# Two halves for the last dense tile of each batch, and other settings for the last five jobs of a planned decoder layer

## The chip, the core and the metric

The kernel runs on one core of a Trainium2 chip. The core has a matrix engine (TensorE, PE in the profile, with its weight loads shown apart as PEld), a vector engine (VectorE, DVE), a scalar engine (ScalarE, ACT), a general engine (GpSimd, POOL) and a queue that issues the transfers here (SyncE, SP). Each engine works through its own list of instructions in order; semaphores tie the lists together. The metric is the device time of one execution in microseconds, as the median of several runs.

## The reference, cut to what matters

The layer works on x of 2 batches by 512 tokens by 1024 features and has three parts, each a residual around a normalised input: an attention with weights cut to their signs, a second attention over a 256-wide stream with a gated block behind it ("xattn"), and a dense layer with low-rank additions ("ffn").

```python
x = x + attn(layernorm(x), ...)
x = x + xattn(layernorm(x), pos, ctx, ...)
x = x + ffn(layernorm(x), gate, kernel, bias, lora_A, lora_B, lora_A_shared, lora_B_shared)

def ffn(x, ...):
    base_out = x @ kernel + bias                    # 1024 x 1024
    A_eff = einsum('bn,nri->bri', gate, lora_A)     # rank 32, mixed per batch
    B_eff = einsum('bn,nor->bor', gate, lora_B)
    delta = B_eff (A_eff x) + lora_B_shared (lora_A_shared x)
    return base_out + delta
```

The change is in the last part and in what precedes it directly. There the output of a tile of 128 tokens is: the normalised tile times the 1024x1024 weights (into which the shared low-rank product is added beforehand), plus the mixed low-rank product, plus the bias, plus the tile itself.

## The kernel before, in words

The kernel is written as some thirty jobs, Python generators that yield one step at a time: an engine, an estimated time, and the moment at which the step's inputs are ready. A planner, `run` (line 453), keeps a clock for each engine and always takes the step with the smallest sum of possible start and lag. The instructions of that step are emitted then, and on each engine they stay in the order in which they were emitted. So the plan fixes the order of all work when the kernel is built; on the chip each instruction then starts when its semaphores allow.

The lag is a priority in microseconds: a job with lag -1.0 is put ahead of a step that could start at the same moment with lag 0.5. The list in `build` (line 1669) gives each job its generator, its lag, and the names that must be finished before it begins. A job's side steps (a copy out of PSUM, a sum, a store) are spawned as jobs of their own, with a lag relative to their parent's: `LAGS` (line 432), looked up first as "job.function" and then as "function", -0.3 if neither is there. `lined` (1205) starts the tiles of a job in order, at most so many at a time, and adds 0.02 of lag per tile.

Buffers are counted in rooms: `take` waits until one is free in the plan, `give` returns it. There are 12 slabs of 8 KB per partition, 4 probs of the same size, 8 pages and 11 rows in SBUF, and 3 pairs (two banks of 512 columns) and 2 single banks in PSUM. At most 3 tail tiles run at once (three lanes). All transfers are issued on SP, in planned order (`fetch`, 535).

The jobs that the change touches, letters A and B standing for batch 0 and 1:

- attC and attD: the second attention of each batch. attC's end gives back three slabs, attD's end three more.
- `factors_back` (job factorsB, 1519): loads the mixed low-rank factors, which an earlier job put into DRAM, into two slabs with six transfers: 1024 KB, 512 KB and four of 128 KB.
- `dense_weights` (job weights, 1536): loads the shared factors and the bias into three pages; then, for each quarter of the 1024x1024 weights, loads 1024 KB into a probs or slab buffer, forms the shared low-rank product of that quarter in two PSUM pairs and adds it on VectorE (`joined`).
- `tails` and `tail` (1369, 1376): for each of four tiles of 128 tokens per batch the rest of the second part: a write of the attention into the stream (`write`, 1257), a read, the gated block (`gated`), a second write, and the addition of the residual, which is loaded again (`residual`). The write has a long chain of small VectorE operations.
- `dense_all` and `dense` (1580, 1583): the third part, tile by tile, two at once per batch. A dense tile begins when weights and factorsB are done and its tail is done. It measures and normalises the tile (VectorE), turns it on TensorE in eight blocks into xt, copies it out, forms the mixed rank product ax, spawns `summed` (which folds the four partial sums of ax), and multiplies into one PSUM pair: 8 products of 512 columns for each of two halves h (each product appears as two records in the profile). Then one rank product for each half closes the pair, one VectorE operation adds the pair to the tile with its bias into a page y, and one transfer of 512 KB stores y.

`SPARE` (446) is read in one place, `attend` (734): in the first attention, the last of four probability tiles of a group is summed directly by TensorE, not added to the others on VectorE first, when VectorE is planned to be busy for longer than SPARE after the product, and always in the last group.

Of the kernel before, what the change touches and what calls it, by code (L numbers as in the profile page):

```python
# [15 lines left out]
ALU = mybir.AluOpType  # L16
AX = mybir.AxisListType

P = 128
NB = 2  # L20
S = 512
NT = S // P
D = 1024
# [46 lines left out]
class Kernel:  # L70
# [354 lines left out]
    def output_weights(self):  # L425
# [6 lines left out]
    LAGS = {  # L432
        "added": 0.0, "ahead": 0.0, "attA.ahead": -0.1, "attA.exponentials": -0.1, "attA.finished": 0.3,
        "attB.added": 0.0, "attB.ahead": -0.3, "co.emptied": -0.1, "cv.emptied": -0.1, "denseA.emptied": -1.0,
        "denseA.summed": -0.6, "denseB.emptied": 0.3, "denseB.summed": -2.0, "emptied": -0.6,
        "exponentials": 0.3, "factor.put": -1.0, "finished": 0.0, "gained": -1.0, "gated": -1.0,
        "joined": -0.6, "k.scale_of": 0.0, "maxA.reduced": 0.0, "maxA.turned": -0.1, "maxB.reduced": 0.3,
        "maxB.turned": -0.3, "maxD.turned": -0.3, "outA.clean": 1.0, "outA.stored": 2.0, "outB.stored": -1.0,
        "proj0.featured": -1.0, "proj0.valued": -0.6, "proj1.featured": -1.0, "proj1.valued": -0.6,
        "q.scale_of": 0.0, "residual": 1.0, "rotated": 0.0, "stateA.emptied": -0.3, "stateA.rotated": -0.1,  # L440
        "stateB.gained": 0.0, "stateB.rotated": 0.0, "stored": 0.6, "summed": -0.6, "tableB.emptied": -2.0,
        "tailA.gained": -1.0, "tailA.residual": -2.0, "tailB.emptied": -0.6, "tailB.gained": -2.0,
        "tailB.gated": -0.6, "tailB.residual": 0.3, "v.scale_of": 0.0, "weights.joined": -0.1,
        "wo.scale_of": 0.0,
    }
    SPARE = 0.5

# [168 lines left out]
    def attend(self, groups, operands, scale, causal):  # L618
# [89 lines left out]
        for n, (g, kt) in enumerate(steps):  # L708
# [23 lines left out]
            else:  # L732

                direct = kt == NT - 1 and (g == groups - 1 or self.free["DVE"] > t + self.SPARE)
                if held is not None and not direct:
# [122 lines left out]
    def stored(self, b, q, x, halves):  # L858
        t = yield from self.join(*halves)
        t = yield from self.fetch(self.kept[b][q][:, :], x, 512, t)  # L860
        self.give("page", t)
        self.when[f"kept{b}{q}"] = t
        return t
# [719 lines left out]
    def dense(self, b, q, tails):  # L1583

        nc = self.io
        weights = yield from self.need("weights", "factorsB")
        t = yield from self.need(f"{tails}.{q}")
        xs = self.tokens(b, q)
        mv, r, t = yield from self.measured([[xs[:, :512], xs[:, 512:]]], t)
        t = max(t, (yield from self.take("page", 2)))  # L1590
        t = yield "DVE", 0.82, t
        xn = self.page([P, D])
        xt = self.page([P, ND, P])
        nc.vector.tensor_scalar(xn, xs, mv[:, 0, 0:1], r, ALU.subtract, ALU.mult)

        def biased(t):
            t = yield "DVE", 1.22, t
            nc.vector.tensor_tensor(xs, xs, self.bias, ALU.add)
            return t

        bias = self.spawn(biased(t), 1.0)
        ends = []
        for g in range(2):
            room = yield from self.take("bank")
            done = yield "PE", 0.62, max(t, room)
            turns = self.transposes(xn, g)
            ends.append(self.spawn(self.emptied("bank", xt[:, 4 * g : 4 * g + 4, :], turns, 512, done)))
        self.give("page", done)
        t = yield from self.join(*ends)
        t = max(t, weights)  # L1610


        r = (NT * b + q) * 32
        slots = [slice(32 * j, 32 * j + 32) for j in (q, q ^ 1)]
        both = slice(64 * (q // 2), 64 * (q // 2) + 64)
        ready = t
        t = max(t, (yield from self.take("row")), (yield from self.take("bank")))
        ax = self.row([P, 2, P])
        t = yield "PE", 0.6, t
        bank = self.bank([P, P])  # L1620
        for i in range(ND):
            j = 32 * (i % 4)
            self.mm(bank[j : j + 32, :], lhsT=self.ae[:, i, r : r + 32], rhs=xt[:, i, :], start=i < 4, stop=i >= 4)

        def summed(bank, t):
            t = yield "DVE", 0.3, t
            nc.vector.tensor_copy(ax[:, 0, :], bank)
            self.give("bank", t)
            t = max(t, (yield from self.take("bank")))
            t = yield "PE", 0.25, t  # L1630
            bank = self.bank([P, P])
            self.mm(bank[both, :], lhsT=self.eyes, rhs=ax[:, 0, :], start=True, stop=True)
            t = yield "DVE", 0.25, t
            nc.vector.tensor_copy(ax[both, 1, :], bank[both, :])
            self.give("bank", t)
            return t

        ranks = self.spawn(summed(bank, t))
        ready = max(ready, (yield from self.take("pair")))
        pair = self.pair()  # L1640
        for h in range(2):
            for i0 in range(0, ND, 2):
                t = yield "PE", 1.82, ready
                for i in range(i0, i0 + 2):
                    self.mm(
                        pair[:, h, :], lhsT=xt[:, i, :], rhs=self.wk[2 * h + i // 4][:, i % 4, :],
                        start=i == 0, stop=False,
                    )
        t = yield "PE", 0.6, max(t, (yield from self.join(ranks)))
        for h in range(2):  # L1650
            self.mm(
                pair[:, h, :], lhsT=ax[slots[h], 1, :], rhs=self.be[slots[h], b, h * 512 : (h + 1) * 512],
                start=False, stop=True,
            )
        self.give("page", t)
        self.give("row", t)
        t = max(t, (yield from self.join(bias)), (yield from self.take("page")))
        t = yield "DVE", 1.22, t
        y = self.page([P, D])
        nc.vector.tensor_tensor(  # L1660
            y.rearrange("p (h n) -> p h n", h=2), pair, xs.rearrange("p (h n) -> p h n", h=2), ALU.add
        )
        self.give("pair", t)
        t = yield from self.fetch(self.out[b * S + q * P : b * S + (q + 1) * P, :], y, 512, t)
        self.give("page", t)
        return t


    def build(self):
# [41 lines left out]
                ("stateB", self.state_inputs(1, False), 0.5, "outB"),  # L1711
                ("factor", self.factors(), -0.5, "maxB.3"),
                ("attC", self.attend_2(0, "maxC"), 0.2, "maxC.0"),
                ("factorsB", self.factors_back(), 5.0, "attD"),
                ("maxD", self.peaks_2(1, "stateB"), 0.5, "stateB", "attC.scores"),
                ("tailW", self.tail_weights(), -0.5, "attC", "stateB"),
                ("tailA", self.tails(0), 0.5, "attC", "tailW"),
                ("attD", self.attend_2(1, "maxD"), 0.2, "maxD.1"),
                ("weights", self.dense_weights(), 0.0, "attD", "attC"),
                ("tailB", self.tails(1), 0.0, "attD", "tailW", "tailA.0"),  # L1720
                ("denseA", self.dense_all(0, "tailA"), 0.5, "tailA.0"),
                ("denseB", self.dense_all(1, "tailB"), 0.2, "tailB.0"),
            ]
        )

# [103 lines left out]
```

## Time and profile before

| what | value |
|---|---|
| median of 3 runs | 1134.14 us (1129.55 to 1135.88) |
| profiled execution | 1131.76 us, of it 1130.0 us of span |
| TensorE | 1050.0 us busy (93%), mean granted clock 0.964 |
| VectorE | 842.0 us busy (75%) |
| ScalarE / GpSimd | 443.7 us (39%) / 239.3 us (21%) |
| DMA | 70.51 MB, mean 62 GB/s |

The span runs from the first to the last instruction in the profile; the rest of the profiled execution's time lies around it. An execution is read by stage: attC ends near 711 us, attD near 845, the dense weights are joined between 849 and 869, and the dense tiles run from 869 to the end, beside the remaining tail tiles. A busy TensorE is not TensorE at full speed: the granted clock tells what share of the full rate it had. Idle time of an engine is named by what ended it, behind an arrow. A row of a timeline has start and duration in us, engine, line, operation, what is written and read, and shapes; L51, L130, L133 and L142 are lines of helpers that record all VectorE, ScalarE and GpSimd operations, matmuls, transposes and transfers, so operations are told apart by the names of their tiles. A tile's name begins with the job that made it: the tokens of batch 0 lie in `tailA_slab` from the tail to the dense stage.

### The profile page before, as it was taken

Reading aid. Unit: us, or ns where it says so; the run is one execution under the profiler, and the core shown is the slowest. Engines: PE = TensorE matmul, PEld = TensorE weight load, DVE = VectorE, ACT = ScalarE, POOL = GpSimd, SP = SyncE. Lnnn points to the kernel's source line nnn. Section 1 sums busy time; section 2 is a strip of 40 time slices with the busy share of each in tenths; the row PEclk is TensorE's granted clock in tenths of the full one; section 3 lists DMA queues with packets and bytes.
Section 4 is the critical chain, followed back from the end, with each engine's and each line's share of the span. In section 5 each row is a group of like instructions: output and inputs, shape, how many; then the busy total and the mean of one; then the engine's idle time right before and its main releaser. Section 6 shows DMA issues by size and latency. Waiting matters only on the chain.

```text
span 1130.0 us, 16083 instructions
## 1 busy us (share of the span) xinstructions
PE 1050.0 (93%) x6331; PEld 520.9 (46%) x6364; DVE 842.0 (75%) x1391; ACT 443.7 (39%) x712; POOL 239.3 (21%) x249
## 2 busy tenths in 40 slices
PE   4889999999999998999999899989987899999897
PEld 3554353333233542332554553546455466675543
DVE  8968888478888866778777972499758778777582
ACT  6763101389600113787221256225753233332310
POOL 3542323412221403264452012001210000000000
PEclk9999999999998897999999899969999899999999
DMA  6621000100213321150022100510143011010100
GB/s 245 213 82 29 20 10 14 35 20 20 66 38 125 137 75 38 26 204 1 17 78 74 49 11 1 187 39 1 47 148 124 0 57 57 23 71 1 56 19 38
DMA packets 25232, 70.51 MB, mean 62 GB/s; under 512 B 5298, under 2 KB 5316, under 8 KB 24260
## 3 DMA queue, kind: packets, MB, share of 16 engines
q1 hardware_dynamic: 25156, 69.48, 18.2%
q8 instruction: 50, 0.82, 0.3%
q14 instruction: 26, 0.21, 0.1%
HBM read 50.59 MB, written 10.49 MB: 54 GB/s over the span
## 4 chain that ended last, share of the span: by engine, by line
PE 77%; DVE 13%; ACT 5%; issue 2%; DMA 1%; POOL 1%; SPq 0%; ACTq 0%; DVEq 0%; POOLq 0%
PE proj_bank L130 9%; PE denseB_pair L130 6%; PE denseA_pair L130 5%; PE outA_bank L130 4%; PE attA_pair L130 4%; PE attB_pair L130 4%; PE attA_bank L130 3%; PE attB_bank L130 3%; PE maxB_pair L130 3%; PE maxA_pair L130 3%; PE tailA_bank L130 3%; PE stateB_bank L130 3%; PE outB_bank L130 3%; PE tailB_bank L130 3%; PE tailA_pair L130 3%; PE factor_bank L130 3%
## 5 line engine op out<-in xcount | busy, mean ns | idle before, releaser
L51 DVE TENSOR_REDUCE maxB_mx<-maxB_pair 128x2 f32<-128x1024 f32 x64 | 75.4, 1218 | 21.4 <-PE maxB_pair L130 21.2
L51 DVE TENSOR_REDUCE maxA_mx<-maxA_pair 128x2 f32<-128x1024 f32 x64 | 75.5, 1216 | 14.1 <-PE maxA_pair L130 14.1
L130 PEld LDWEIGHTS <-start_slab 128*128 128x128 bf16 x480 | 45.0, 99 | 69.3 <-issue 22.2
L51 DVE TENSOR_TENSOR attB_probs<-attB_probs,attB_probs 128x1024 f32<-128x1024 f32 x46 | 62.7, 1401 | 13.0 <-ACT attB_probs L51 8.2
L51 ACT ACTIVATE attB_probs<-attB_pair 128x1024 f32<-128x1024 f32 x64 | 62.6, 1022 | 20.3 <-PE attB_pair L130 10.2
L51 DVE TENSOR_TENSOR attA_probs<-attA_probs,attA_probs 128x1024 f32<-128x1024 f32 x46 | 56.7, 1283 | 16.9 <-ACT attA_probs L51 15.9
L51 ACT ACTIVATE attA_probs<-attA_pair 128x1024 f32<-128x1024 f32 x64 | 62.1, 1021 | 9.8 <-PE attA_pair L130 9.4
L130 PE MATMUL proj_bank<-in_slab,start_slab 128*128 128x512 bf16 x230 | 55.6, 386 | 2.1 <-ACT in_slab L51 1.2
L130 PE MATMUL proj_bank<-in_probs,start_slab 128*128 128x512 bf16 x232 | 53.8, 380 | 0.6 <-issue 0.3
L130 PE MATMUL maxB_pair<-maxB_row,proj_slab 32*128 32x512 f32 x256 | 47.4, 687 | 3.2 <-DVE maxB_mx L51 3.1
L51 POOL TENSOR_SCALAR proj_row<-proj_row 128x512 f32<-128x512 f32 x24 | 48.1, 2005 | 1.9
L130 PE MATMUL outA_bank<-wo_slab,attA_slab 128*128 128x512 bf16 x183 | 46.8, 401 | 1.4 <-ACT maxB_shift L51 0.7
L130 PE MATMUL attB_pair<-proj_slab,attB_row 32*128 32x512 f32 x256 | 46.9, 686 | 0.0
L51 ACT ACTIVATE proj_row<-proj_bank,cs 128x512 f32<-128x512 f32 x20 | 13.7, 687 | 81.6 <-PE proj_bank L130 61.0
L130 PE MATMUL outB_bank<-wo_slab,attB_slab 128*128 128x512 bf16 x186 | 42.6, 379 | 0.7 <-POOL attB_slab L51 0.3
L130 PE MATMUL attA_pair<-proj_slab,attA_row 32*128 32x512 f32 x256 | 41.6, 639 | 0.3 <-ACT attA_probs L51 0.3
L130 PE MATMUL attB_bank<-attB_probs,proj_slab 128*32 128x512 f32 x256 | 37.6, 619 | 1.1 <-DVE tableA_slab L51 0.7
L51 ACT COPY maxB_shift<-maxB_bank 128x512 bf16<-128x512 bf16 x8 | 4.7, 586 | 86.4 <-PE maxB_bank L133 86.4
L51 POOL TENSOR_SCALAR proj_slab<-proj_row 128x512 f32<-128x512 f32 x24 | 14.7, 614 | 108.6 <-ACT proj_row L51 89.1
L130 PE MATMUL maxA_pair<-maxA_row,proj_slab 32*128 32x512 f32 x256 | 36.8, 640 | 0.1
L51 POOL TENSOR_SCALAR_AFFINE_SELECT attD_probs<-attD_probs 128x512 f32<-128x512 f32 x16 | 12.0, 750 | 114.7 <-ACT attD_probs L51 105.2
L51 POOL MEMSET tailB_row<- 9x128 f32 x8 | 1.6, 195 | 160.8 <-DVE tailB_page L51 103.6
(411 smaller groups left out, 2311.8 us busy)
## 6 DMA issues: line engine op xcount, KB each, us to landing
in_page<-in_x_dram SPq DMA_DIRECT2D x8, 512.0 KB, 4.4
q_page<-in_q_weight_dram SPq DMA_DIRECT2D x8, 512.0 KB, 5.1
wo_page<-in_o_weight_dram SPq DMA_DIRECT2D x8, 512.0 KB, 3.4
tailW_slab<-in_write_dram SPq DMA_DIRECT2D x3, 752.0 KB, 7.1
maxA_row<-proj_slab SPq DMA_DIRECT2D x32, 64.0 KB, 2.0
attA_row<-proj_slab SPq DMA_DIRECT2D x32, 64.0 KB, 2.0
maxB_row<-proj_slab SPq DMA_DIRECT2D x32, 64.0 KB, 2.0
outA_page<-in_x_dram SPq DMA_DIRECT2D x4, 512.0 KB, 3.8
```

Of the source, the lines that this page charges most:

```text
L51: return self.kernel.pin(getattr(self.engine, name)(*args, **kw))
L130: self.pin(self.nc.tensor.matmul(*args, **kw))
```

## The change

In `dense`, the tile q = 3 of each batch is finished in two halves of 512 columns. After the 8 products of the first half, its rank product follows at once (before, both rank products came after all 16), and a spawned step `stored` adds that half to the tile and stores it with a transfer of 256 KB; the same follows for the second half. The sum of the ranks (`summed`) must therefore be there before the second half's products, which stand behind it. The other three tiles of each batch are finished as before, except that in all tiles the page y is taken before the page of xt is given back.

Beside it stand new settings. In `LAGS`: denseA.stored 1.0 and denseB.stored -2.0 (new), denseB.summed -0.1 for -2.0, tailB.gated 0.0 for -0.6. `SPARE` 1 for 0.5. In the list of jobs: factorsB needs attC, not attD, with lag 20.0 for 5.0; weights has lag -1.0 for 0.0 and needs only attD; tailB has lag 0.2 for 0.0 and needs tailA.1 in the place of tailA.0; denseB has lag 0.5 for 0.2.

```diff
     LAGS = {
...
-        "denseA.summed": -0.6, "denseB.emptied": 0.3, "denseB.summed": -2.0, "emptied": -0.6,
+        "denseA.stored": 1.0, "denseA.summed": -0.6, "denseB.emptied": 0.3, "denseB.stored": -2.0,
+        "denseB.summed": -0.1, "emptied": -0.6, "exponentials": 0.3, "factor.put": -1.0, "finished": 0.0,
...
-        "tailB.gated": -0.6, "tailB.residual": 0.3, "v.scale_of": 0.0, "weights.joined": -0.1,
+        "tailB.emptied": -0.6, "tailB.gained": -2.0, "tailB.gated": 0.0, "tailB.residual": 0.3,
...
-    SPARE = 0.5
+    SPARE = 1
...
         ready = max(ready, (yield from self.take("pair")))
         pair = self.pair()
+        y = None
+        ends = []
+
+        def stored(h, t):
+            cols = slice(h * 512, (h + 1) * 512)
+            t = yield "DVE", 0.69, t
+            nc.vector.tensor_tensor(y[:, cols], pair[:, h, :], xs[:, cols], ALU.add)
+            return (yield from self.fetch(self.out[b * S + q * P : b * S + (q + 1) * P, cols], y[:, cols], 256, t))
+
         for h in range(2):
             for i0 in range(0, ND, 2):
                 t = yield "PE", 1.82, ready
...
-        t = yield "PE", 0.6, max(t, (yield from self.join(ranks)))
-        for h in range(2):
-            self.mm(
-                pair[:, h, :], lhsT=ax[slots[h], 1, :], rhs=self.be[slots[h], b, h * 512 : (h + 1) * 512],
-                start=False, stop=True,
-            )
+            split = q == NT - 1
+            if not h and not split:
+                continue
+            ready = t = yield "PE", 0.6, max(t, (yield from self.join(ranks)))
+            for k in [h] if split else range(2):
+                self.mm(
+                    pair[:, k, :], lhsT=ax[slots[k], 1, :], rhs=self.be[slots[k], b, k * 512 : (k + 1) * 512],
+                    start=False, stop=True,
+                )
+            if y is None:
+                room = max((yield from self.join(bias)), (yield from self.take("page")))
+                y = self.page([P, D])
+            if split:
+                ends.append(self.spawn(stored(h, max(t, room))))
         self.give("page", t)
         self.give("row", t)
-        t = max(t, (yield from self.join(bias)), (yield from self.take("page")))
-        t = yield "DVE", 1.22, t
-        y = self.page([P, D])
-        nc.vector.tensor_tensor(
-            y.rearrange("p (h n) -> p h n", h=2), pair, xs.rearrange("p (h n) -> p h n", h=2), ALU.add
-        )
-        self.give("pair", t)
-        t = yield from self.fetch(self.out[b * S + q * P : b * S + (q + 1) * P, :], y, 512, t)
+        if not ends:
+            t = yield "DVE", 1.22, max(t, room)
+            nc.vector.tensor_tensor(
+                y.rearrange("p (h n) -> p h n", h=2), pair, xs.rearrange("p (h n) -> p h n", h=2), ALU.add
+            )
+            self.give("pair", t)
+            t = yield from self.fetch(self.out[b * S + q * P : b * S + (q + 1) * P, :], y, 512, t)
+        else:
+            t = yield from self.join(*ends)
+            self.give("pair", t)
         self.give("page", t)
         return t
...
-                ("factorsB", self.factors_back(), 5.0, "attD"),
+                ("factorsB", self.factors_back(), 20.0, "attC"),
...
-                ("weights", self.dense_weights(), 0.0, "attD", "attC"),
-                ("tailB", self.tails(1), 0.0, "attD", "tailW", "tailA.0"),
+                ("weights", self.dense_weights(), -1.0, "attD"),
+                ("tailB", self.tails(1), 0.2, "attD", "tailW", "tailA.1"),
                 ("denseA", self.dense_all(0, "tailA"), 0.5, "tailA.0"),
-                ("denseB", self.dense_all(1, "tailB"), 0.2, "tailB.0"),
+                ("denseB", self.dense_all(1, "tailB"), 0.5, "tailB.0"),
```

## The prediction

> **What bounds the kernel now.** I read the page first, for the whole span.
>
> ```profile
> PE 1050.0 (93%) x6331; PEld 520.9 (46%) x6364; DVE 842.0 (75%) x1391; ACT 443.7 (39%) x712; POOL 239.3 (21%) x249
> PE 77%; DVE 13%; ACT 5%; issue 2%; DMA 1%; POOL 1%; SPq 0%; ACTq 0%; DVEq 0%; POOLq 0%
> ```
>
> TensorE is busy 93% of the time and carries 77% of the chain that ended last. The change adds no TensorE work and takes none away, so it can only close holes, undo a lowered clock, or shorten what follows the last matmul. It cannot act before batch 0's second attention (attC) ends, near 711 us: until then the same jobs compete with the same settings (SPARE is dealt with below). So I next read the stretches from 700 us on, in pieces of 5 us, for holes.
>
> ```profile
> 861.00:866.00 5.00, 5.00 (x23) 2.70 (x21) 3.89 (x9) 1.10 (x3) 0.00 (x0) 1.00 0.00 0
> 866.00:871.00 5.00, 2.72 (x25) 1.94 (x17) 4.90 (x9) 2.27 (x6) 0.00 (x0) 1.00 0.01 3
> 871.00:876.00 5.00, 2.23 (x8) 1.43 (x8) 4.93 (x9) 0.69 (x2) 0.00 (x0) 0.54 0.00 0
> 876.00:881.00 5.00, 4.05 (x21) 2.06 (x22) 3.81 (x9) 1.63 (x2) 0.00 (x0) 0.50 0.00 0
> ```
>
> The columns are length, busy PE, weight loads, DVE, ACT, POOL, then granted clock, DMA share and GB/s. From 866 to 881 PE has its largest hole, and the clock falls to half. TensorE's order of work names who ends it.
>
> ```profile
> 872.95 1.12 PE L133 MATMUL denseA_bank<-ident,denseA_page 128*128 128x128 f32 x4 [3.77 <-DVE denseA_page L51]
> 874.75 1.12 PE L133 MATMUL denseA_bank<-ident,denseA_page 128*128 128x128 f32 x4 [0.68 <-ACT denseA_page L51]
> ...
> 878.65 3.44 PE L130 MATMUL denseA_pair<-weights_probs,denseA_page 128*128 128x512 f32 x4
> ```
>
> PE waits for the first dense tile to be normalised. VectorE's order and the DMA queue's order show why that is late.
>
> ```profile
> 866.61 2.35 DVE L51 TENSOR_TENSOR weights_slab<-weights_pair,weights_slab 128x1024 f32<-128x1024 f32 x2
> 868.88 1.28 DVE L51 BATCH_NORM_STATS2 denseA_st<-tailA_slab 128x6 f32<-128x512 f32 x2
> ...
> 872.09 0.81 DVE L51 TENSOR_SCALAR denseA_page<-tailA_slab,denseA_mv,denseA_rstd 128x1024 f32<-128x1024 f32 x1
> ```
> ```profile
> 835.95 2.31 SPq L142 DMA_DIRECT2D weights_probs<-in_kernel_dram  x2
> 838.31 3.83 SPq L142 DMA_DIRECT2D factorsB_slab<-factor  x6
> 842.19 2.00 SPq L142 DMA_DIRECT2D weights_slab<-in_kernel_dram  x2
> ```
>
> The tile's statistics start only behind the last two joins of the dense weights, though its input was finished by the add at 817.40. The loads of those last weights stand behind the six loads of factorsB. The end of the kernel is the third place.
>
> ```profile
> 1123.88 1.13 PE L130 MATMUL denseA_pair<-factorsB_slab,denseA_row 32*128 32x512 f32 x4
> 1125.06 1.23 DVE L51 TENSOR_TENSOR denseA_page<-denseA_pair,tailA_slab 128x1024 f32<-128x1024 f32 x1 [14.70 <-PE denseA_pair L130]
> 1126.31 0.33 SPq L142 DMA_DIRECT2D out_dram<-denseA_page  x1
> ```
>
> After the last matmul nothing overlaps: 1.23 for the add, then the store.
>
> **The change part by part.** SPARE, 0.5 to 1. It could only turn a direct sum of probabilities into an added one.
>
> ```profile
> L130 PE MATMUL attA_bank<-attA_probs,ones x72: 592/592/617, 233.6 to 304.3; 128*32 128x512 f32 x72
> ```
>
> Each of 8 groups needs 4 sums, two records each: 64. The 8 extra are one direct group, the forced last one; attB has 72 too. No free choice was direct at 0.5, so none is at 1: zero.
>
> The loads of factorsB move from attD's end (845) to attC's (711). They carry 2.1 MB (1024, 512 and 4 of 128 KB). The stretches 841 to 846 and 851 to 856 ran at 406 and 392 GB/s, so they occupy 2.1/0.40 = 5.2 us. At the new place DMA is busy to 725 (share 0.56 to 0.99), then idle to 755 (0.00 or 0.01): with lag 20 they fall there. Put before the tail's loads they would delay the first normalising on ACT (724.9) by 5.2 us, whose result DVE reads only at 749.6: cover 20 us, cost zero. Six issues on SP, 3.83, pass an SP queue that waits. The two slabs taken earlier bring the count to exactly 12 of 12 (tail weights 3, batch 0's tokens 2, both attention outputs 2, batch 1's state 3, factors 2): nothing is turned away.
>
> The weights, with these loads out of their way and a lag of -1.0 for 0.0, can join up to 5.2 us earlier, and with them the first dense tile. Bounds: nothing, if DVE is the true limit; at most the holes from 868 to 881, 0.46+3.77+0.68+0.68+0.41 = 6.0, plus the clock. That costs 3.2: the transposes took 1.12 twice against 0.66 at 900.50 and 901.94; the rank products 1.08 and 0.69 against 0.65 and 0.43; the first four pair products 3.44 against 1.88. So 0 to -9.2. I take the transfer, 5.2, which is the delay that goes, and half of the clock, 1.6, since 0.8 us of hole would stay: -6.8. Late next: the tail tile whose VectorE chain ran from 862 to 877 then meets the joins earlier.
>
> The split of tile 3. Its additions: two DVE adds of 512 columns at 0.69 (the row for 128x512 operands) for one at 1.22, of which one, with its store, lies beside the second half's 7.03 us of matmuls; one more SP issue at 0.34, on a waiting queue. At the end, 1.23 becomes 0.69: -0.54. The store of 512 KB landed in 2.6; 256 KB (the factors' stores) in a median of 2.3: -0.3. Together -0.8 (bounds -0.5, if landing does not shrink, and -1.1, by the fastest of the factors' transfers, 2.0). The Trainium skill, "DMA: Bandwidth & Descriptors", section on the anatomy of one DMA, gives about 2 us fixed plus the bytes at 436 GB/s for GpSimd's path; that would make the halving worth an estimated 0.6 for 0.3, and the sum 0.3 lower. The rows are of this kernel's own SP queue, so I keep them.
>
> The first half's rank product now stands before the second half and waits for the rank sum; behind it on PE stand 16 matmuls. For the last tile the sum was there at 1110.35 and is needed at 1116.9. For denseB.3 it was there at 1091.07 and is needed at 1098.9; with denseB.summed at -0.1 for -2.0 it may fall behind the chain that fills DVE to 1099.69 and cost some 2 us. Bounds 0 and +2; I take 0, nearer to the 7 us of slack. The output page is now taken before the transposed one is given back: if all 8 are out, the add waits, at worst a store's landing, 2.6; the PSUM pairs (3) cover it: 0.
>
> The priorities (tailB 0.0 to 0.2, its start after tailA.1, denseB 0.2 to 0.5, gated 0.0). tailB's first tile already waits for tailA.1's lane, so its start hardly moves. tailB still stands before tailA and dense. From 1042 to 1110 PE's holes add up to 7.4 and its lowered clock to 3.2 (two first halves of 8.83 and 8.40 for 7.03): best case -10.6. Worst case is the second rival, +17.4. I take 0, since the order of jobs stays nearly the same.
>
> Sum, on the profiled execution's 1131.76 (span 1130.0 and 1.8 around it): -6.8-0.8 = 1124.2. The shown median, 1134.14, is 2.4 above it, so 1126.5.
>
> **The rivals.** First, the hole was DVE's: from 866 to 876 DVE is busy 9.83 of 10, and the eight joins of 1.22 come with every order. Then only the split pays: 1133.3. Against it: DVE had 3.9 us idle between 851 and 866 in which joins could have gone.
>
> Second, slower: at the end a tail's last chain loses its cover. After its second write a tail runs from 1067.10 to 1090.67 before its dense pair begins; today another dense tile's 16.3 us (1090.67 to 1106.97) lie beside such a chain.
>
> ```profile
> 1067.10 0.59 PE L130 MATMUL tailA_bank<-tailW_slab,tailA_row 9*128 9x256 f32 x2
> ...
> 1089.22 0.43 PE L130 MATMUL denseB_bank<-denseB_page,factorsB_slab 128*32 128x128 f32 x8 [1.88 <-DVE denseB_page L51]
> ...
> 1090.67 8.40 PE L130 MATMUL denseB_pair<-weights_probs,denseB_page 128*128 128x512 f32 x16
> ```
>
> If the raised denseB lag or the later gated steps leave both last tails to end after all other dense tiles, 16.3 go bare, and 1.1 of clock: +17.4, 1143.9. It decides from 13.3 us of lost cover on (the 7.6 gained plus 0.5%). For it: tailA.3 was ready at 901 and its second write ran at 1042, so the end already hangs on lags. Against it: tailA.3 now competes with denseB at 0.5, not 0.2.
>
> Third, the handovers close as well: about 8 of the 10.6 go, 1118.5. The Trainium skill, "TensorE: Matmul & The Clock Gate", section on the HAM clock gate, has the clock fall only after an idle window of some 3.4 us; by it the gaps here (the longest 1.88) cost no clock, and at most 7.4 were to be had. The trace differs: from 1090 to 1095 the granted clock was 0.67.
>
> **How the numbers follow.** The forecast 0.52 (own range 1121 to 1131), DVE-bound 0.20, lost cover 0.16, handovers 0.12. A measurement tells about 0.5%, 5.7 us, from no change: faster is below 1128.5. The third case and four fifths of the first make 0.56; the rest of the first and the DVE case 0.27; lost cover 0.17 with the odd rest. The range 1117 to 1141 leaves out most of the lost cover and the best of the handovers, under 2 in 10.
>
> **What would show it.** Right: factorsB's loads before 760 and none between the weights' four; the last join before 865; no 3.77 hole before the first dense transposes and a clock of 1.0 after it; 72 sums; a last add of 0.69 with a store of 256 KB. Wrong: the joins still end at 868, or PE has a hole of over 10 us after 1040.

## The result, and the profile after

The changed kernel takes 1128.32 us in the median of 13 runs (1124.53 to 1133.02), the kernel before 1133.13 in 13 runs beside it (1129.55 to 1136.85). The ratio is 0.9962, with a 95% interval of 0.9947 to 0.9976: by the ratio some 4.3 us faster. The time lies inside the predicted range and the sign is the predicted one, but the gain is little more than half of the 7.6 us forecast, and by the bound of 0.5% it counts as no change.

The page of the changed kernel, busy times and chain:

```profile
PE 1056.2 (94%) x6364; PEld 520.5 (46%) x6364; DVE 840.2 (75%) x1391; ACT 443.9 (39%) x714; POOL 238.2 (21%) x249
PE 78%; DVE 13%; ACT 5%; issue 2%; DMA 1%; POOL 1%; SPq 0%; DVEq 0%; ACTq 0%; POOLq 0%
```

Of TensorE's 1056.2 us against 1050.0 only a part can be new work: busy time also grows at a lowered clock, and the page before misses 33 records.

The two profiled executions, 1127.92 and 1131.76 us, need care. Up to attD's last write to `attD_slab` the four compute engines execute the same instructions in the same order in both kernels; only SP's order differs, where from 620 us on the loads of factorsB stand ahead of those of the tail's weights. Yet that write ends at 844.3 after and at 847.3 before: 3.0 of the 3.8 us lie ahead of the changed part. In the fourteen profiled executions here its end lies between 844.3 and 849.8, so this is read as what one execution differs from another. So stages are counted from that write. The stretches from it, of before and then of after, end with the last matmul (columns: length, busy PE, weight loads, DVE, ACT, POOL, granted clock, DMA share, GB/s):

```profile
847.30:947.30 100.00, 88.69 (x458) 55.26 (x459) 79.65 (x151) 32.69 (x66) 0.78 (x4) 0.95 0.17 58
947.30:1047.30 100.00, 98.54 (x473) 61.00 (x472) 77.75 (x152) 32.07 (x65) 0.97 (x5) 1.00 0.10 36
1047.30:1125.00 77.70, 70.19 (x278) 35.73 (x276) 41.03 (x74) 13.22 (x28) 0.00 (x0) 0.96 0.10 34
```
```profile
844.30:944.30 100.00, 93.27 (x499) 59.40 (x500) 80.30 (x152) 35.25 (x71) 1.17 (x6) 0.98 0.13 43
944.30:1044.30 100.00, 94.50 (x415) 55.90 (x415) 77.14 (x159) 32.17 (x66) 0.58 (x3) 0.90 0.10 36
1044.30:1122.50 78.20, 76.31 (x293) 38.73 (x291) 39.40 (x67) 11.10 (x24) 0.00 (x0) 1.00 0.08 31
```

What TensorE loses in a stretch is its length less busy time times clock (about, since the clock is a mean):

| us after attD's last write | lost before | lost after | difference |
|---|---|---|---|
| 0 to 100 | 15.7 | 8.6 | -7.1 |
| 100 to 200 | 1.5 | 15.0 | +13.5 |
| 200 to the last matmul | 10.3 | 1.9 | -8.4 |
| sum | 27.5 | 25.5 | -2.0 |
| matmul work (shown below) | | | +2.1 |
| after the last matmul | 5.0 | 3.7 | -1.3 |

The forecast gain is there in the first row; a second, larger one towards the end is more than paid back by a new stall in the middle; and the shorter end is more than eaten by new matmul time. The pair of executions gives -1.2 by this account and -0.8 by its ends (282.7 and 281.9 us after the write). That is less than the ratio's -4.3; single executions of one kernel lie up to 8.5 us apart in the runs above. The rows tell where time moved, the ratio how much in all.

The first stage, TensorE's order of work in the kernel before and then in the changed one:

```profile
848.05 7.31 PE L130 MATMUL tailA_pair<-tailA_row,tailW_probs 128*128 128x128 f32 x64
...
860.18 5.32 PE L130 MATMUL tailA_bank<-tailW_slab,tailA_page 128*128 128x376 f32 x16
865.43 1.14 PE L130 MATMUL weights_pair<-weights_page,weights_page 32*128 32x512 f32 x8
```
```profile
845.04 3.74 PE L130 MATMUL tailA_pair<-tailA_row,tailW_probs 128*128 128x128 f32 x32
848.70 1.14 PE L130 MATMUL weights_pair<-weights_page,weights_page 32*128 32x512 f32 x8
851.21 3.84 PE L130 MATMUL tailA_pair<-tailA_row,tailW_probs 128*128 128x128 f32 x32 [0.37 <-DVE weights_probs L51]
...
857.44 2.26 PE L130 MATMUL weights_pair<-weights_page,weights_page 32*128 32x512 f32 x8 [0.73 <-DVE weights_slab L51]
...
860.57 5.27 PE L130 MATMUL tailA_bank<-tailW_slab,tailA_page 128*128 128x376 f32 x16
...
867.78 0.63 PE L133 MATMUL denseA_bank<-ident,denseA_page 128*128 128x128 f32 x4
...
872.43 5.07 PE L130 MATMUL denseA_pair<-weights_probs,denseA_page 128*128 128x512 f32 x8
```

VectorE's order and the SP queue's, of the same kernel:

```profile
859.75 2.35 DVE L51 TENSOR_TENSOR weights_slab<-weights_pair,weights_slab 128x1024 f32<-128x1024 f32 x2
862.01 1.28 DVE L51 BATCH_NORM_STATS2 denseA_st<-tailA_slab 128x6 f32<-128x512 f32 x2
```
```profile
619.83 3.85 SPq L142 DMA_DIRECT2D factorsB_slab<-factor  x6
...
832.95 2.30 SPq L142 DMA_DIRECT2D weights_probs<-in_kernel_dram  x2
835.31 1.05 SPq L142 DMA_DIRECT2D weights_slab<-in_kernel_dram  x2
```

The last join ends at 862.1 (17.8 us after the write, 21.6 before), the hole of 3.77 ahead of the first dense transposes is gone, and these take 0.63 for 1.12. The clock is 1.00 until 869, but 0.78 from 869 to 874: the drop is shorter than before, not gone.

Two things changed in the order. The second low-rank product of the weights (848.70) now stands between the two halves of the tail's 64 small products, which were one block of 7.31 us ahead of it. But by the third product this lead has shrunk to 0.7 us (10.7 after the write, at 854.98, for 11.4). What brings the last join forward is the fourth product: it now starts at 857.44, ahead of the tail's 16 products of 5.27 us; before, it stood behind them and started at 865.43. That is 13.1 after the write for 18.1.

The loads of factorsB went out at 620, not after 720: their two slabs were free that early.

The end, on TensorE, VectorE and SP:

```profile
1112.38 1.12 PE L130 MATMUL denseB_pair<-factorsB_slab,denseB_row 32*128 32x512 f32 x2
1113.54 0.69 DVE L51 TENSOR_TENSOR denseB_page<-denseB_pair,tailB_slab 128x512 f32<-128x512 f32 x1 [6.11 <-PE denseB_pair L130]
...
1114.29 7.13 PE L130 MATMUL denseB_pair<-weights_slab,denseB_page 128*128 128x512 f32 x16 [0.79 <-DVE denseB_page L51]
1121.35 1.12 PE L130 MATMUL denseB_pair<-factorsB_slab,denseB_row 32*128 32x512 f32 x2
1122.51 0.69 DVE L51 TENSOR_TENSOR denseB_page<-denseB_pair,tailB_slab 128x512 f32<-128x512 f32 x1 [8.28 <-PE denseB_pair L130]
```

The last addition is 0.69 as forecast. But TensorE waits 0.79 for the first half's addition before it begins the second half, and each half has a rank product of 1.12, where both halves together took 1.13 before.

The middle, stretches and TensorE's order:

```profile
985.00:990.00 5.00, 5.00 (x23) 2.38 (x23) 2.71 (x7) 1.29 (x3) 0.00 (x0) 0.50 0.60 210
1015.00:1020.00 5.00, 3.37 (x11) 1.21 (x10) 4.75 (x11) 0.37 (x1) 0.19 (x1) 0.86 0.00 0
1030.00:1035.00 5.00, 3.88 (x40) 2.20 (x38) 3.67 (x9) 2.77 (x5) 0.00 (x0) 0.50 0.32 108
```
```profile
1018.54 0.37 PE L133 MATMUL tailB_bank<-ident,tailB_few 128*8 128x128 f32 x1 [1.63 <-ACT tailB_row L51]
...
1035.27 9.00 PE L130 MATMUL denseB_pair<-weights_probs,denseB_page 128*128 128x512 f32 x16
```

No single hole is long, but there are several, and the clock falls to half more than once, so that 7.03 us of products take 9.00. One thing that moved into this stretch is seen in the VectorE rows of tile `tailA_slab` between 960 and 1110, of before and then of after (min/median/max duration in ns, first and last start):

```profile
L51 DVE TENSOR_TENSOR tailA_slab<-tailA_slab,tailA_page x2: 631/928/1226, 1097.8 to 1098.4; 128x256 f32<-128x256 f32 x1, 128x1024 f32<-128x1024 f32 x1
```
```profile
L51 DVE TENSOR_TENSOR tailA_slab<-tailA_slab,tailA_page x2: 625/920/1214, 1000.4 to 1003.4; 128x256 f32<-128x256 f32 x1, 128x1024 f32<-128x1024 f32 x1
```

Batch 0's last tail tile ends its second write 156 us after attD's write, not 250. Its chain now runs in the middle, beside those of two tiles of batch 1, all on VectorE, and is missing at the end, where TensorE has less to wait for. That this meeting is the cause of the stall is not shown; the runs below speak against it as the only one.

### The profile page after: what moved, and what is told of

Its sections match the earlier page's. It is cut to its first block, busy times and chain, and to the rows that moved or that the text cites. A ratio compares the mean times of both kernels' runs of the same rounds, so it can differ in the third digit from the quotient of the medians.

```text
span 1126.2 us, 16121 instructions
## 1 busy us (share of the span) xinstructions
PE 1056.2 (94%) x6364; PEld 520.5 (46%) x6364; DVE 840.2 (75%) x1391; ACT 443.9 (39%) x714; POOL 238.2 (21%) x249
## 4 chain that ended last, share of the span: by engine, by line
PE 78%; DVE 13%; ACT 5%; issue 2%; DMA 1%; POOL 1%; SPq 0%; DVEq 0%; ACTq 0%; POOLq 0%
PE proj_bank L130 8%; PE denseA_pair L130 6%; PE denseB_pair L130 5%; PE outA_bank L130 4%; PE attA_pair L130 4%; PE attB_pair L130 4%; PE tailA_bank L130 4%; PE attA_bank L130 3%; PE attB_bank L130 3%; PE maxB_pair L130 3%; PE maxA_pair L130 3%; PE outB_bank L130 3%; PE stateB_bank L130 3%; PE tailB_bank L130 3%; PE factor_bank L130 3%; PE tailA_pair L130 2%
## 5 line engine op out<-in xcount | busy, mean ns | idle before, releaser
L130 PEld LDWEIGHTS <-start_slab 128*128 128x128 bf16 x480 | 45.0, 99 | 69.8 <-issue 22.9
L51 POOL TENSOR_SCALAR outA_row<-outA_row 128x512 f32<-128x512 f32 x16 | 21.4, 1340 | 65.0 <-DVE outA_row L51 60.8
```

Of the source, the lines that this page charges most:

```text
L51: return self.kernel.pin(getattr(self.engine, name)(*args, **kw))
L130: self.pin(self.nc.tensor.matmul(*args, **kw))
```

## The experiments

In the table the ratio is to the kernel before in the same session, and "last join", "last matmul" and "end" are us after attD's last write in the profiled execution (before: 21.6, 277.7, 282.7; after: 17.8, 278.2, 281.9).

| run | ratio (interval) | last join | last matmul | end |
|---|---|---|---|---|
| split_only | 1.0035 (1.0018 to 1.0053) | 21.6 | 284.1 | 287.9 |
| settings_only | 1.0008 (0.9991 to 1.0025) | 17.8 | 281.9 | 286.9 |
| fac_wt | 1.0162 (1.0134 to 1.0191) | 17.8 | 297.3 | 302.3 |
| tail_only | 1.0010 (0.9994 to 1.0026) | 21.6 | 280.6 | 285.6 |
| whole_tile | 0.9954 (0.9933 to 0.9975) | 17.8 | 275.9 | 280.9 |
| page_only | 1.0003 (0.9983 to 1.0022) | 21.6 | 278.0 | 283.0 |
| after_two_pairs | 1.0025 (1.0006 to 1.0045) | 17.8 | 282.8 | 286.6 |
| split_two_pairs | 1.0023 (1.0005 to 1.0041) | 21.6 | 282.0 | 285.7 |
| whole_no_fac | 0.9953 (0.9932 to 0.9974) | 17.8 | 275.1 | 280.1 |
| whole_no_wt | 1.0015 (1.0002 to 1.0028) | 21.6 | 280.7 | 285.7 |
| whole_no_tail | 1.0173 (1.0149 to 1.0196) | 17.8 | 299.5 | 304.5 |
| late_halves | 0.9943 (0.9926 to 0.9961) | 17.8 | 277.1 | 281.5 |

### One part at a time

The new code of `dense` alone, with the two new lags of `stored` and all other settings of before (split_only):

```diff
+            split = q == NT - 1
...
+            if split:
+                ends.append(self.spawn(stored(h, max(t, room))))
```

> The kernel before with the split of the last tiles alone (with the two new lags of stored), all other settings as before. Theory 1 (the gain is the earlier weights; the split pays back what it saves): within 1 us of before, a ratio of 0.999 to 1.001; the last add is 0.69 us and the last store 256 KB, but PE stands still for about 0.8 us ahead of the second half's products, ended by the add of the first half. Theory 2 (the gain is the new order of the last tails and dense tiles): also within 1 us. Theory 3 (the split itself is the gain): 0.8 us faster or more, and no such hole.

It is slower by 0.35%, some 4 us. TensorE's order at the end of this run:

```profile
1107.65 5.42 PE L130 MATMUL denseB_pair<-weights_slab,denseB_page 128*128 128x512 f32 x12 [0.79 <-DVE denseB_page L51]
...
1123.64 1.12 PE L130 MATMUL denseA_pair<-factorsB_slab,denseA_row 32*128 32x512 f32 x2
1124.69 1.98 PE L130 MATMUL denseA_pair<-weights_slab,denseA_page 128*128 128x512 f32 x4
1127.46 5.42 PE L130 MATMUL denseA_pair<-weights_slab,denseA_page 128*128 128x512 f32 x12 [0.79 <-DVE denseA_page L51]
```

In both tiles the second half's products break off and wait 0.79 for the first half's addition. The two halves write different banks, but they are two parts of one tile `pair` in PSUM. Where the wait stands in the second half depends on how far TensorE had come in the plan when the addition was emitted. What else the split costs is worked out below.

All settings, with the code of `dense` as before (settings_only):

```diff
-                ("factorsB", self.factors_back(), 5.0, "attD"),
+                ("factorsB", self.factors_back(), 20.0, "attC"),
...
-                ("weights", self.dense_weights(), 0.0, "attD", "attC"),
+                ("weights", self.dense_weights(), -1.0, "attD"),
...
-                ("denseB", self.dense_all(1, "tailB"), 0.2, "tailB.0"),
+                ("denseB", self.dense_all(1, "tailB"), 0.5, "tailB.0"),
```

> The changed kernel with its dense stage as before, so all new settings and no split. Theory 1 and theory 2: as fast as the changed kernel, ratio 0.995 to 0.998. Theory 3: 0.8 us or more slower than the changed kernel, ratio above 0.998.

No difference can be measured, although the joins end at 17.8. What was gained there and towards the end was lost in the middle: by the same reckoning as above TensorE loses 22.9 us there (15.0 in the changed kernel, 1.5 before). One wait of 5.12 us stands in it, which the changed kernel doesn't have:

```profile
995.44 0.38 PE L133 MATMUL tailA_bank<-ident,tailA_few 128*8 128x128 f32 x1 [5.12 <-ACT tailA_row L51]
```

The two settings that are to bring the weights forward, alone (fac_wt; the first two changed lines of the diff above):

> The kernel before with the new settings of factorsB and weights alone. Theory 1: 3 to 5 us faster, ratio 0.9955 to 0.9975; the last join of the weights ends some 18.5 us after attD's last write (22.3 before) and the first dense product starts 29 us after it (32.0 before). Theory 2: the same earlier first product, but no gain at the end, ratio 0.999 to 1.001.

This is the slowest but one of all, 1.6% or some 18 us slower than before. TensorE's and VectorE's order in this run:

```profile
1087.34 0.66 PE L130 MATMUL denseB_bank<-denseB_page,factorsB_slab 128*32 128x128 f32 x8 [11.31 <-DVE denseB_page L51]
```
```profile
1081.51 0.96 DVE L51 TENSOR_TENSOR tailB_slab<-tailB_page,tailB_page 128x768 f32<-128x768 f32 x1
...
1086.65 0.64 DVE L51 COPY denseB_page<-denseB_bank 128x512 f32<-128x512 f32 x1
```

The last tail's chain runs bare: from 1075 to 1090 TensorE is busy 2.85 of 15 us, at a clock of 0.67. Dense tiles are left, and one of them is turned already, but the copy for which TensorE waits stands behind that chain in VectorE's order. That is what the second rival feared, a chain without cover, though it comes by VectorE's order and not because no dense tile was left.

It isn't the whole of the 18 us. By the reckoning above TensorE loses 16.1 us in the second 100 (1.5 before) and 19.5 after them (10.3 before), and some 5 less in the first. The 15 us around the bare chain hold 13.1 of the 19.5; so the stall in the middle costs more than the lost cover.

The priorities of the tail and dense jobs alone (tail_only):

```diff
-        "denseA.summed": -0.6, "denseB.emptied": 0.3, "denseB.summed": -2.0, "emptied": -0.6,
+        "denseA.summed": -0.6, "denseB.emptied": 0.3, "denseB.summed": -0.1, "emptied": -0.6,
...
-        "tailB.gated": -0.6, "tailB.residual": 0.3, "v.scale_of": 0.0, "weights.joined": -0.1,
+        "tailB.gated": 0.0, "tailB.residual": 0.3, "v.scale_of": 0.0, "weights.joined": -0.1,
...
-                ("tailB", self.tails(1), 0.0, "attD", "tailW", "tailA.0"),
+                ("tailB", self.tails(1), 0.2, "attD", "tailW", "tailA.1"),
...
-                ("denseB", self.dense_all(1, "tailB"), 0.2, "tailB.0"),
+                ("denseB", self.dense_all(1, "tailB"), 0.5, "tailB.0"),
```

> The kernel before with the new settings of tailB, denseB, denseB.summed and tailB.gated alone. Theory 1: within 2 us of before, ratio 0.998 to 1.002, first dense product 32 us after attD's last write as before. Theory 2: 3 to 5 us faster, ratio 0.9955 to 0.9975, and PE's holes after 1040 add up to 4 us or less where they were 7.

No difference can be measured. The stall in the middle comes with this part alone too: TensorE loses 10.0 us there, against 1.5 before. So no part gains alone, one loses 1.6%, another 0.35%, and the whole gains 0.4%: the parts don't add, since each shifts the order in which all the others are planned. SPARE alone, 1 for 0.5, gives the same lists of instructions on every engine as before, so it has no part in this.

### What the split costs

The changed kernel with every tile whole; what is left of the new code is that the output page is taken before the page of xt is given back (whole_tile):

```diff
-            split = q == NT - 1
+            split = False
```

> The changed kernel with no tile split, so with its settings and with its new order of taking the page y; its lists of instructions differ from the changed kernel's only in the last tile's end (some 33 rows on PE, none before). Theory 1 (the split pays back in a wait what it saves): as the changed kernel within 1 us, ratio 0.995 to 0.998; the last add is 1.22 us and the store 512 KB, but the 0.79 us hole ahead of the second half is gone. Rival, the split is what made the combination faster than its settings alone: ratio 0.999 to 1.002. The difference from the kernel with the settings alone (1.0008) is then that of the page's order.

The changed kernel without its split is at least as fast: 0.9954 beside 0.9962, which the intervals don't tell apart. In the profiles the whole tile's last matmul comes 2.3 us earlier and its end 1.0 earlier. The end of this run:

```profile
1121.02 1.13 PE L130 MATMUL denseB_pair<-factorsB_slab,denseB_row 32*128 32x512 f32 x4
1122.20 1.23 DVE L51 TENSOR_TENSOR denseB_page<-denseB_pair,tailB_slab 128x1024 f32<-128x1024 f32 x1 [12.99 <-PE denseB_pair L130]
1123.45 0.33 SPq L142 DMA_DIRECT2D out_dram<-denseB_page  x1
```

Both rank products, four records, take 1.13. This kernel differs from settings_only in nothing but the moment at which the page is taken, and gains 0.5% where that gained nothing. So a detail that adds no work decides whether the plan has the wait of 5.12.

The same detail on the kernel before (page_only): the new code of `dense` with `split = False`, and all settings as before.

> The kernel before with the page y taken before the page of xt is given back, no split and no new setting. If the 0.35% loss of the split alone is made by the halves (holes of 1.59, 0.79 and 0.79 at the end), this one is within 0.1% of before; if it is made by the page's order, it is 0.3% slower.

Alone it does nothing: 1.0003.

Two runs give the second half of tile 3 a PSUM pair of its own, so that nothing in PSUM ties it to the first half's addition; one with all settings (after_two_pairs), one with the settings of before (split_two_pairs):

```diff
         pair = self.pair()
+        halves = [pair, pair]
+        if q == NT - 1:
+            ready = max(ready, (yield from self.take("pair")))
+            halves[1] = self.pair()
...
-                        pair[:, h, :], lhsT=xt[:, i, :], rhs=self.wk[2 * h + i // 4][:, i % 4, :],
+                        halves[h][:, h, :], lhsT=xt[:, i, :], rhs=self.wk[2 * h + i // 4][:, i % 4, :],
```

> The changed kernel, in which the second half of a split tile is made in a PSUM pair of its own. Theory 1 (PE waits because both halves lie in one tile and the add of the first is ordered ahead of the second half's products): no hole ended by the add ahead of the second half, and 0.8 to 1.2 us less after attD's last write than the changed kernel (281.9), ratio 0.9945 to 0.997. Rival, the hole is of the chip (reading one bank holds up writing the other): the hole of about 0.8 stays.

> The kernel before with the split alone and a PSUM pair of its own for each half. Theory 1: the two holes of 0.79 go, the hole of 1.59 ahead of the last tile's transposes may stay; 1 to 3 us less than the split alone (1.0035), ratio 1.000 to 1.0025. Rival, the loss lies elsewhere: ratio 1.003 or more.

TensorE's order at the end of split_two_pairs:

```profile
1119.84 1.12 PE L130 MATMUL denseA_pair<-factorsB_slab,denseA_row 32*128 32x512 f32 x2
1120.89 7.13 PE L130 MATMUL denseA_pair<-weights_slab,denseA_page 128*128 128x512 f32 x16
```

The waits of 0.79 are gone, so the shared PSUM tile was their cause. Yet the kernel stays 0.23% slower than before. A lone rank product holds TensorE for 1.05 us (1119.84 to 1120.89), against 1.06 for both together (1103.12 to 1104.18 in whole_tile): 2 x 1.05 = 2.1 us of matmul time in two split tiles, more than the 1.3 that the shorter end saves. A second cost stays as well: in both runs with the settings of before the plan puts the last tile's first transposes between the two halves of denseB.3, where they wait for the normalised page, 1.59 us in split_only and 1.55 here, with the second half behind them. These terms come to about the measured losses: 2.1 - 1.3 + 1.55 = 2.4 us here, for 0.23% or 2.6, and with the two waits of 0.79 some 4.0 in split_only, for 0.35% or 4.0.

With all settings the separate pair is worse (1.0025). TensorE's order in after_two_pairs:

```profile
1111.61 1.94 PE L133 MATMUL denseB_bank<-ident,denseB_page 128*128 128x128 f32 x8 [3.67 <-DVE denseB_page L51]
```

The plan around the last tile comes out otherwise with it: no other products are left to stand beside its normalising, and TensorE waits 3.67 for it.

So the last one keeps both rank products together at the end, and halves only what follows them, the addition and the store of tile 3 (late_halves, from whole_tile):

```diff
-        if not ends:
+        if q == NT - 1:
+            ends = [self.spawn(stored(h, max(t, room))) for h in range(2)]
+            t = yield from self.join(*ends)
+            self.give("pair", t)
+        elif not ends:
```

> whole_tile, in which the last tile of each batch has both rank products at the end as before, and only its add and its store are made in two halves. Theory: the two rank products take 1.1 us together, as in the whole tile, where the split has 1.1 for each; no hole ended by an add ahead of a product of the same tile; from PE's end to the last instruction 4.3 to 4.6 us, where the whole tile has 5.0 and the split 3.7. Time within 1 us of whole_tile, ratio 0.993 to 0.997.

```profile
1122.83 1.13 PE L130 MATMUL denseB_pair<-factorsB_slab,denseB_row 32*128 32x512 f32 x4
1124.01 1.29 DVE L51 TENSOR_TENSOR denseB_page<-denseB_pair,tailB_slab 128x512 f32<-128x512 f32 x2 [12.26 <-PE denseB_pair L130]
1124.72 0.93 SPq L142 DMA_DIRECT2D out_dram<-denseB_page  x2
```

The lines are its end. The first store is issued behind the first addition, and from the last matmul to the end it takes 4.4 us (5.0 whole, 3.7 split) with no matmul time added. Its ratio, 0.9943, is the best of all; its interval lies clear of 1, but it is not told apart from the changed kernel or whole_tile by these intervals.

### What brought the weights forward, and what guards the end

Three runs take one part of the settings back from whole_tile. The loads of factorsB back to their old place (whole_no_fac):

```diff
-                ("factorsB", self.factors_back(), 20.0, "attC"),
+                ("factorsB", self.factors_back(), 5.0, "attD"),
```

> The changed kernel with whole last tiles (whole_tile, 0.9954), and factorsB set back to attD and lag 5.0. If the earlier loads of factorsB bring the weights forward: the six loads stand among the weights' loads again, the last join ends 21 to 22 us after attD's last write (17.8 with the change), the first dense product starts 31 us after it (28.7), and the ratio rises to 0.998 to 1.000. If the lag of weights does it alone: 17.8 and 28.7 stay, and the ratio too.

and the weights back to their old lag (whole_no_wt):

```diff
-                ("weights", self.dense_weights(), -1.0, "attD"),
+                ("weights", self.dense_weights(), 0.0, "attD", "attC"),
```

> whole_tile with weights set back to lag 0.0. If the earlier loads of factorsB bring the weights forward, most of it stays: last join 18 to 20 us after attD's last write, first dense product 28 to 30, ratio 0.995 to 0.999. If the lag does it: 21.6 and 31.3, as before, ratio 0.998 to 1.001.

The first changes nothing (0.9953): the six loads go out at 815.9, later than in whole_tile but still ahead of the weights' four. The second loses the whole gain (1.0015). TensorE's order and the SP queue's in whole_no_wt:

```profile
862.24 5.32 PE L130 MATMUL tailA_bank<-tailW_slab,tailA_page 128*128 128x376 f32 x16
867.49 1.14 PE L130 MATMUL weights_pair<-weights_page,weights_page 32*128 32x512 f32 x8
...
875.00 1.12 PE L133 MATMUL denseA_bank<-ident,denseA_page 128*128 128x128 f32 x4 [3.77 <-DVE denseA_page L51]
```
```profile
838.02 2.31 SPq L142 DMA_DIRECT2D weights_probs<-in_kernel_dram  x2
840.38 1.05 SPq L142 DMA_DIRECT2D weights_slab<-in_kernel_dram  x2
```

Here no load of factorsB stands between the weights' four, and still the joins end at 21.6 and the hole of 3.77 is back: the fourth low-rank product stands behind the tail's 16 products again, as before. So transfers out of the way bring the joins no further without the lag. The lag with the old transfers in between was not run, but the trace of before tells what they could have held up: its last two loads of weights were issued at 842.2 and 843.8 and landed 11.9 and 13.0 later, 6.8 and 9.5 us after attD's write. The changed kernel joins these two quarters from 11.9 and 15.4 on, so even loads as late as before's would have been in time.

The priorities of tail and dense back (whole_no_tail; the diff of tail_only reversed, on whole_tile):

> whole_tile with tailB, denseB, denseB.summed and tailB.gated set back. Theory: the first 100 us after attD's last write stay as they are in whole_tile (first dense product at 28.7), but a last tail's chain loses its cover at the end, as in the run with the settings of factorsB and weights alone: a PE hole of more than 5 us later than 200 us after attD's last write, ratio 1.005 to 1.017. Rival: these settings have no part in the gain, ratio 0.994 to 0.998.

1.0173, with a wait of 10.93 on TensorE 233.6 us after the write, like fac_wt's. The earlier weights alone expose the last tail; the priorities avoid it, and they bring nothing without the weights. The stall in the middle they don't avoid: TensorE loses 16.4 us there without them and 15.0 with them (whole_tile).

## Why the prediction was right or wrong

**The weights, -6.8.** The size was right: TensorE loses 7.1 us less in the first 100 us. The cause given was not, so the agreement is luck. The step said that 5.2 us of transfers out of the way would let the weights join earlier; whole_no_wt has them out of the way and gains nothing, whole_no_fac has the old setting of the factors and gains all, and the last join came 3.8 us earlier, not 5.2. What held it was TensorE's own order, the fourth low-rank product behind the tail's 16 products of 5.32 us; with the lag of -1.0 it goes ahead of them. The working had this lag in one half-sentence and gave it no price. The sign "a clock of 1.0 after it" came in part: 0.78 from 869 to 874.

**The first rival, a limit set by VectorE,** fell with it: the last join came 3.8 us earlier and the tile's statistics followed at once.

**The loads of factorsB, zero,** was right, but they went out at 620, as the slabs were free before attC ended. SPARE, zero, was right: 72 sums.

**The split, -0.8.** The terms at the end were right in kind and too small: the end after the last matmul shrank by 1.3. The addition gave the 0.54 forecast; the last store landed 2.0 after its issue for 2.6, so 0.6 was gained where 0.3 was taken, as the estimate set beside it had said. The step that failed is "The change adds no TensorE work". Two rank products in two row groups run side by side when they follow one another, and the split parts them: +1.05 in each of two tiles. It could have been seen: eight products of 512 columns took 7.03, 0.88 each, so two in sequence should have taken 1.76, and the row said 1.13 for both. The wait for the first half's addition, 0.79 and 0.35, was missed as well: the working asked what the rank sum delays, not what the addition's reading of half a PSUM tile delays. The rank sum itself, bounded by 0 and +2, came in time, as taken.

**The priorities, zero.** Bounds of -10.6 and +17.4 were given and zero taken, "since the order of jobs stays nearly the same". That sentence failed: batch 0's last tail tile finishes 94 us earlier. The third rival's gain came, -8.4 against the 8 of its forecast, and 13.5 us were lost in the middle, for which no case was made. What causes this stall stays open. It isn't that tile's chain alone: fac_wt and whole_no_tail lose 16.1 and 16.4 us in the same stretch, although there the tile ends its second write only some 228 and 230 us after attD's. It comes with the earlier weights alone and with the priorities alone (10.0 in tail_only), and with neither in page_only (1.5).

**The second rival** didn't come, but was no idle bound: in two of the twelve kernels a last tail's chain ran bare, and they are 1.6 and 1.7% slower than before. Its price of 17.4 was not too low: 13.1 us were lost around the bare chain in fac_wt, and the stall in the middle cost more than that. It was one part of the settings away.

**The sum.** -6.8 - 0.8 was forecast and -4.3 measured. In the pair of profiles the two forecast terms come out at -7.1 and -1.3; what was left out is +5.1 from the stall in the middle less the gain at the end, and +2.1 of matmul time. That adds to -1.2, less than the ratio shows, and which of the rows is smaller in the typical execution stays open. That the time fell inside the range of the forecast case is thus in part luck: two terms of 13.5 and 8.4, for which zero was taken, went against each other.

## What to carry to other kernels

When a step moves a small product away from its neighbour, look up whether the two ran side by side before calling the move free: a row that holds both is not twice the price of one. Where a planner orders all work, a setting's effect is read from what it stands behind on the engine, and settings must be tried together and with each one taken back, since none of these gained alone. Halving an output shortens what follows the last matmul (4.4 us for 5.0 here) if only the addition and the store are halved; halves in one PSUM tile that the next products still write made TensorE wait here. And a size that comes out right doesn't show that the cause was: only the settings taken back one by one told which of them had moved the joins.

## What the runs showed of the hardware

The pairing of the rank products: four records of 32x512 in two row groups hold TensorE for 1.06 us, two in one row group for 1.05. The Trainium skill, "TensorE: Matmul & The Clock Gate", Part 3 on packing small matmuls, says that products of 32 rows in distinct row groups run concurrently; the rows here agree (line 1614 of the kernel puts the two products at rows of q and of q with its last bit flipped). The same page of the Trainium skill, under "Why this matters for your kernels", has a single one take as long as one of 128 rows; here it took 1.05, and one of 128 rows 0.88. By the Trainium skill the split's price could have been estimated: 0.88 more in each split tile, 1.8 for the 2.1 measured.

The clock fell to half without a long hole. Two stretches of the changed kernel:

```profile
981.00:984.00 3.00, 1.40 (x10) 0.89 (x9) 2.94 (x7) 1.33 (x3) 0.00 (x0) 1.00 0.01 3
984.00:987.00 3.00, 3.00 (x21) 1.39 (x20) 2.92 (x7) 0.96 (x2) 0.00 (x0) 0.57 0.31 82
```

In the first TensorE was busy for 1.40 of 3 us, in pieces, with no hole above 0.93; in the second it had no hole at all, and ran at 0.57, then at 0.50 to 990. The Trainium skill's same page, Part 1, has the clock fall after an idle window of about 3.4 us; none stands ahead of this drop. Whether a window that is half idle is enough, or the short transposes in it count for less, these runs can't tell.

The end after the last matmul with a store of 512 KB took 5.0 us, with 256 KB behind an addition of 0.69 it took 3.7; of the 1.3 between them 0.54 is the addition and 0.6 the shorter landing (2.0 us for 256 KB, 2.6 for 512 KB), more than the 0.3 that the median of other 256 KB transfers had suggested.
